# Differential attention and routed experts: the scores of four head groups made in one step, two score tiles at a time

## The chip, the cores and the metric

The kernel runs on one core of a Trainium2 chip. The metric is device time in microseconds (us) for one launch. Three runs of the kernel before took 1216.85, 1217.22 and 1220.14 us, so its median is 1217.22 us.

The engines are named as the profile names them: PE is TensorE with its matmuls, PEld is TensorE's weight load, DVE is VectorE, ACT is ScalarE, POOL is GpSimd and SP is SyncE. PSUM is the memory that TensorE writes its products into.

## The reference

The input x is 8 sequences of 512 tokens with 128 features. One layer of attention with 16 heads of 8 features makes two score matrices per head, takes two softmaxes, subtracts one from the other and divides by the sum of absolute values. A residual and a layer norm follow. Then each token goes to the best two of 8 experts, again with a residual and a norm.

```python
q = _split_heads(x @ Wq.T); k1 = _split_heads(x @ Wk1.T); k2 = _split_heads(x @ Wk2.T)
s1 = jnp.einsum('bhqd,bhkd->bhqk', q, k1) * SCALE
s2 = jnp.einsum('bhqd,bhkd->bhqk', q, k2) * SCALE
attn_exp, attn_noise = softmax(causal(s1)), softmax(causal(s2))
attn = attn_exp - sigmoid(lambda_logit) * attn_noise
attn = attn / jnp.maximum(jnp.sum(jnp.abs(attn), -1, keepdims=True), 1e-06)
out = jnp.einsum('bhqk,bhkd->bhqd', attn, v)
...
h = jax.nn.silu(jnp.einsum('btd,edf->betf', xn, W1))
y = jnp.einsum('betf,efd->betd', h, W2)
out = jnp.einsum('bte,betd->btd', wdense, y)
```

## The kernel before

**Units.** The attention is cut into 128 units: 8 batches, and in each 16 blocks of 32 queries (class `Unit`, L294). Block j sees L = 32(j+1) keys. The 16 heads lie in four groups g of 32 rows; the four heads of a group, times 32 queries, fill the 128 partitions of a result. A unit has eight score matrices of 128 x L, one for each group and each of the two key sets s.

**Slots.** The scores of a unit are made in slots, each with its own PSUM tile `sc` of 128 x 2 x 512 float32, from a pool of two (`ps_s`, L121). For L up to 256 (early units, tiles named sc_None in the profile) a slot is one pair of groups with both key sets, and a unit has two. For L above 256 (late units, tiles named sc) a slot is one pair of groups with one key set, and a unit has four. `scores` (L312) issues two products for a slot (L327), each of which uses 32 rows of TensorE, and two small products that add the causal mask (L336). Each product in float32 shows as two records in the profile.

**The way of a unit.** `maxima` (L345) takes the negated maximum of a slot on DVE (L349 early, L357 late). `exps` (L361) makes the exponentials on ACT into the tile `et` (L367), with their sums. `ratios` (L375) makes the factor c2 from the sums, three small DVE instructions. `combine` (L385) takes one piece of the unit: DVE finds the larger of the two softmaxes for the sum of absolute values (L393), and POOL scales the second set by -c2 (L403) and gathers leftover blocks (L417). `transposes` (L439) turns and adds both sets on PE into the single PSUM tile `pt` (L448). `evacuate` (L458) copies it with ACT (L473). `times_v` (L480) multiplies by the values on PE (L490). After each fourth unit `block_tasks` (L498) copies the sums of products (L508), normalises, projects and adds the residual.

**Order.** The order on every engine is written out by hand: the engines take instructions in the order in which Python issues them. `round_of` (L1083) is one round, for the slot `now`; it issues the scores of the next slot, `ahead`, and moves every unit that is on its way by one step. Steps that have been queued run in it at fixed places: `on_act` on ACT, `on_dve` and `on_dve_late` on DVE, `on_pool`, `moves` and `gathers` on POOL. Its last part issues tasks of other work: `misc` (projections of the next batch, L236, and the steps of a block), `routing`, and the experts (`turn`, L866; `hidden`, L897). How many expert tasks are issued follows from a counter `due`, which grows by a modelled time of the round (L1131 to L1140), not from a clock.

The order inside a round before the change, cut short:

```python
after_blocks(...)                                   # times_v of finished units
ahead["sc"] = ahead["u"].scores(ahead["slot"])
v.evacuate(piece, pt); run(on_act)
now["u"].maxima(now["slot"], now["sc"])
v.transposes(piece); run(on_dve)
v.combine(piece)
now["u"].exps(now["slot"], now["sc"])
```

**After the attention**, rounds without a slot drain what is left: expert tiles, the dense experts of the last two blocks, gathers and the output.

Of the kernel before, what the change touches and what calls it, by code (L numbers as in the profile page):

```python
# [9 lines left out]
F32 = mybir.dt.float32  # L10
# [10 lines left out]
def kernel(  # L21
# [16 lines left out]
    P = 128  # L38
    B, T, D = x.shape
# [4 lines left out]
    Q = 32  # L44
# [67 lines left out]
    with ExitStack() as actx:  # L112
# [181 lines left out]
        class Unit:  # L294


            def __init__(self, b, j, blk):
                self.b, self.j, self.blk = b, j, blk
                self.L = (j + 1) * Q
                self.n = -(-self.L // P)  # L300
                self.i, self.jj = j // JT, j % JT

                self.early = self.L <= T // 2
                self.slots = [(gp, None) for gp in range(2)] if self.early else [
                    (gp, s) for gp in range(2) for s in range(2)
                ]
                self.pieces = [(0, 1), (2, 3)] if self.early else [(g,) for g in range(NG)]
                self.nm = sp.tile([P, NG, 2], F32, tag="nm", name=f"nm_{b}_{j}")
                self.et = ep.tile([P, NG, 2, T], F32, tag="et", name=f"et_{b}_{j}")
                self.aT = self.c2 = self.rest = None  # L310

            def scores(self, slot):  # L312
                gp, s = slot
                qb, kT = qkv[self.b][:2]
                L, j = self.L, self.j
                sc = ps_s.tile([P, 2, T], F32, tag="sc", name=f"sc_{self.b}_{j}_{gp}_{s}")

                if s is None:
                    parts = [sc[:, gi].rearrange("p (s l) -> p s l", s=2) for gi in range(2)]
                    sets = slice(0, 2)  # L320
                else:
                    parts = [sc[:, gi : gi + 1] for gi in range(2)]
                    sets = slice(s, s + 1)
                ns = sets.stop - sets.start
                for gi in range(2):
                    r = slice(32 * (2 * gp + gi), 32 * (2 * gp + gi) + 32)
                    nc.tensor.matmul(  # L327
                        parts[gi][:, :, :L],
                        lhsT=qb[r, j].rearrange("p h q -> p (h q)"),
                        rhs=kT[r, sets, :L],  # L330
                        start=True,
                        stop=False,
                    )
                for gi in range(2):
                    r = slice(32 * (2 * gp + gi), 32 * (2 * gp + gi) + 32)
                    nc.tensor.matmul(  # L336
                        parts[gi][:, :, L - Q : L],
                        lhsT=i4[r].rearrange("p h q -> p (h q)"),
                        rhs=mk[r].unsqueeze(1).to_broadcast([32, ns, Q]),
                        start=False,  # L340
                        stop=True,
                    )
                return sc

            def maxima(self, slot, sc):  # L345
                gp, s = slot
# [38 lines left out]
            def combine(self, piece):  # L385

                if self.c2 is None:
                    self.ratios()  # L390
                L = self.L
                for g in piece:
                    nc.vector.scalar_tensor_tensor(  # L393
# [649 lines left out]
                step()  # L1043

        misc, routing, experts, moves, gathers = (deque() for _ in range(5))
        to_combine, to_transpose, to_evacuate, to_multiply = deque(), deque(), deque(), deque()

        def after_blocks(u):
            u.times_v()
# [10 lines left out]
        def time_of(width):  # L1060

            return (0.5 + width / 1024) / 1.5
# [17 lines left out]
        pace = due = now_at = 0.0  # L1080
        attention_done = False

        def round_of(now=None, ahead=None):  # L1083

            nonlocal due, now_at
            for _ in range(len(to_multiply)):
                after_blocks(to_multiply.popleft())
            if ahead:  # L1090
                ahead["sc"] = ahead["u"].scores(ahead["slot"])
            for _ in range(len(to_evacuate)):
                v, piece, pt = to_evacuate.popleft()
                v.evacuate(piece, pt)
                if piece[-1] == NG - 1:
                    to_multiply.append(v)
            run(on_act)
            if now:
                now["u"].maxima(now["slot"], now["sc"])
            for _ in range(len(to_transpose)):  # L1100
                v, piece = to_transpose.popleft()
                to_evacuate.append((v, piece, v.transposes(piece)))
            run(on_dve)
            left = now["left"] if now else 2
            for _ in range(-(-len(to_combine) // left)):
                v, piece = to_combine.popleft()
                v.combine(piece)
                to_transpose.append((v, piece))
            if now:
                now["u"].exps(now["slot"], now["sc"])  # L1110
                if now["left"] == 1:
                    to_combine.extend((now["u"], piece) for piece in now["u"].pieces)
            run(on_dve_late)
            room = 2
            if misc:
                misc.popleft()()
                room -= 1
            if routing:
                step = routing.popleft()
                step()  # L1120
                room -= step.__name__ == "counts"


            for _ in range(1 if now else 2):
                if on_pool:
                    on_pool.popleft()()
                elif moves:
                    moves.popleft()()
                elif gathers and (now or not misc and not routing):
                    gathers.popleft()()  # L1130
            if now:  # L1131
                spent = time_of(2 * now["u"].L * (2 if now["slot"][1] is None else 1))
                now_at += spent
                due += spent * pace
            else:
                due += 2
            while due >= 1 and experts and room:
                experts.popleft()()
                due -= 1
                room -= 1  # L1140
            due = min(due, 4.0)

        with tc.manual_schedule(
# [57 lines left out]
                        zero.unsqueeze(1).to_broadcast([P, c.nt, D]),  # L1201
                    )

            last = None
            for b in range(B):
                for j in range(NJ):
                    if j % JT == 0:
# [7 lines left out]
                    if b + 1 < B and j == 8:  # L1215
                        misc.extend(projection_tasks(b + 1))
                    u = Unit(b, j, blk)
                    for k, slot in enumerate(u.slots):
                        ahead = {"u": u, "slot": slot, "left": len(u.slots) - k}
                        if last is None:  # L1220
                            ahead["sc"] = u.scores(slot)
                        else:
                            round_of(last, ahead)
                        last = ahead
            round_of(last)
            attention_done = True
            while (
                to_combine or to_transpose or to_evacuate or to_multiply
                or misc or routing or experts or moves or gathers or on_act or on_dve or on_dve_late or on_pool
            ):  # L1230
                round_of()
# [49 lines left out]
```

## Time and profile before

| | us |
|---|---|
| three runs | 1216.85, 1217.22, 1220.14 |
| profiled execution, own time | 1212.04 |
| span of that execution's trace | 1210.1 |
| PE busy | 1093.9 |
| DVE busy | 927.1 |
| ACT busy | 780.4 |
| POOL busy | 526.8 |
| mean granted TensorE clock | 0.927 of full speed |

The durations below come from the profiled execution, so sums are made against its time, 1212.04 us, of which the trace covers 1210.1 us. It lies 0.4% below the median of the three runs. A busy PE is not PE at its peak, since matmuls are pipelined and their ends are modelled in the trace.

In a group of instructions of the profile, `out<-in` names the tiles, then come the shapes, the count, the busy time in us, the mean duration of one in ns, and the idle time of the engine just before these instructions with what ended most of it. In a timeline each line has its start in us, its length in us, the engine, the line of code and the operation; a count behind x means that many records merged in one line. Windows give, for each stretch, the busy time of PE, PEld, DVE, ACT and POOL with instruction counts, and then the granted clock, the busy share of the DMA engines and GB/s.

### The profile page before, as it was taken

How to read it: one execution, taken by the hardware profiler on the slowest of the kernel's cores; microseconds unless marked ns; L12 is line 12 of the kernel's file. 1: busy time of each engine (PE TensorE's matmuls, PEld its weight loads, DVE VectorE, ACT ScalarE, POOL GpSimd, SP SyncE). 2: the span in 40 equal slices, each digit the busy share in tenths (PEclk: the TensorE clock that was granted, in tenths of full speed). 3: DMA queues.
4: the chain of work that ended last, by engine and by line, in shares of the span. 5: the costliest groups of instructions: out<-in, count | busy, mean ns of one | idle time of the engine just before them, and what ended most of it. 6: DMA issues, size and time to landing. Idle time of an engine off the chain costs nothing.

```text
span 1210.1 us, 28192 instructions
## 1 busy us (share of the span) xinstructions
PE 1093.9 (90%) x9450; PEld 776.2 (64%) x9450; DVE 927.1 (77%) x2837; ACT 780.4 (64%) x2775; POOL 526.8 (44%) x935
## 2 busy tenths in 40 slices
PE   5999899989999899989998999988999989997686
PEld 3566565555666566666666666666667667777675
DVE  4688778777887887987887878887767898874556
ACT  3678767576777777766766867774567566662221
POOL 4343433463423442267464432333554652444333
PEclk7699969797999999989998999997899799998998
DMA  4400000110221112100322222221213344444762
GB/s 133 122 8 1 10 2 8 31 56 30 50 63 46 54 32 67 45 27 27 93 69 58 73 54 68 64 73 31 81 52 91 95 120 124 122 123 129 207 177 67
DMA packets 128895, 84.28 MB, mean 70 GB/s; under 512 B 22896, under 2 KB 114288, under 8 KB 128752
## 3 DMA queue, kind: packets, MB, share of 16 engines
q1 hardware_dynamic: 111952, 68.26, 20.2%
q0 software_dynamic: 3840, 7.87, 2.3%
q10 hardware_dynamic: 12960, 6.36, 1.8%
q8 instruction: 75, 1.23, 0.4%
q14 instruction: 68, 0.56, 0.2%
HBM read 63.31 MB, written 17.56 MB: 67 GB/s over the span
## 4 chain that ended last, share of the span: by engine, by line
PE 60%; DVE 16%; ACT 11%; issue 6%; POOL 4%; DMA 3%; ACTq 1%; POOLq 0%; SPq 0%; DVEq 0%
PE pt L448 19%; PE sc L327 13%; ACT et L367 7%; PE po L490 5%; PE pz L900 5%; PE pa L880 5%; PE sc_None L327 5%; DVE junk L393 2%; DVE nm L357 2%; PE pmo L541 2%; ACT aT L473 2%; DVE nm L349 2%; POOL et L403 1%; DVE hT L847 1%; POOL xs L777 1%
## 5 line engine op out<-in xcount | busy, mean ns | idle before, releaser
L403 POOL TENSOR_SCALAR et<-et,c 128x224 f32<-128x224 f32 (+15 forms) x512 | 270.9, 534 | 458.1 <-DVE junk L393 295.0
L448 PE MATMUL pt<-ident,et 128*128 128x128 f32 (+1 forms) x2048 | 326.7, 296 | 26.8 <-ACT aT L473 14.9
L448 PEld LDWEIGHTS pt<-ident,et 128*128 128x128 f32 (+1 forms) x2048 | 230.5, 145 | 159.6 <-issue 58.2
L367 ACT ACTIVATE et<-sc,nm 128x512 f32<-128x512 f32 (+7 forms) x512 | 300.4, 595 | 48.7 <-DVE nm L357 27.6
L357 DVE TENSOR_REDUCE nm<-sc 128x2 f32<-128x576 f32 (+7 forms) x256 | 252.0, 984 | 45.1 <-PE sc L336 44.6
L473 ACT COPY aT<-pt 128x384 f32<-128x384 f32 (+5 forms) x488 | 186.1, 407 | 134.5 <-PE pt L448 130.7
L393 DVE SCALAR_TENSOR_TENSOR junk<-et,c 128x224 f32<-128x224 f32 (+15 forms) x512 | 258.6, 505 | 9.6
L327 PE MATMUL sc<-kT,qb 32*128 32x384 f32 (+7 forms) x1024 | 246.8, 559 | 10.9 <-ACT et L367 9.6
L367 ACT ACTIVATE et<-sc_None,nm 128x256 f32<-128x256 f32 (+7 forms) x512 | 188.6, 387 | 32.0 <-DVE nm L349 22.0
L327 PE MATMUL sc_None<-kT,qb 32*128 32x512 f32 (+7 forms) x512 | 116.5, 535 | 21.8 <-ACT et L367 21.0
L900 PE MATMUL pz<-xgT,w 128*128 128x128 f32 x704 | 102.1, 291 | 18.8 <-DVE xgT L874 18.5
L349 DVE TENSOR_REDUCE nm<-sc_None 128x4 f32<-128x256 f32 (+7 forms) x128 | 96.1, 751 | 29.6 <-PE sc_None L336 29.3
L327 PEld LDWEIGHTS sc<-kT,qb 32*128 32x128 f32 x1024 | 78.3, 187 | 61.3 <-ACT et L367 27.4
L367 ACT ACTIVATION_READ_ACCUMULATOR et<-sc_None,nm 128x1 f32 x512 | 108.1, 211 | 0.0
L900 PEld LDWEIGHTS pz<-xgT,w 128*128 128x128 f32 x704 | 92.5, 204 | 23.6 <-DVE xgT L874 21.2
L367 ACT ACTIVATION_READ_ACCUMULATOR et<-sc,nm 128x1 f32 x512 | 103.9, 203 | 0.0
L880 PE MATMUL pa<-w,hT 128*128 128x128 f32 x704 | 98.1, 285 | 0.6 <-ACT ysb L890 0.6
L845 ACT ACTIVATE th<-pz 128x512 f32<-128x512 f32 x88 | 52.7, 599 | 68.9 <-PE pz L900 47.9
L880 PEld LDWEIGHTS pa<-w,hT 128*128 128x128 f32 x704 | 90.9, 202 | 1.3 <-ACT ysb L890 0.7
L777 POOL DMA_INDIRECT xs<-xh,row x60 | 65.9, 1099 | 46.9 <-DMA xs<-xh,row 31.3
L490 PE MATMUL po<-aT,vt 128*32 128x128 f32 (+1 forms) x2048 | 85.3, 290 | 0.0
L847 DVE SCALAR_TENSOR_TENSOR hT<-th,pz 128x512 f32<-128x512 f32 x88 | 60.2, 684 | 30.8 <-ACT th L845 30.6
(150 smaller groups left out, 1281.0 us busy)
## 6 DMA issues: line engine op xcount, KB each, us to landing
w<-in_w_dram SPq DMA_DIRECT2D x192, 256.0 KB
xg<-xs SPq DMA_DIRECT2D x88, 64.0 KB
ys<-ysb ACTq DMA_DIRECT2D x88, 64.0 KB
xs<-zero SPq DMA_DIRECT2D x2, 1600.0 KB
xs<-zero SPq DMA_DIRECT2D x2, 1216.0 KB
xt<-in_x_dram SPq DMA_DIRECT2D x8, 256.0 KB
out_dram<-ot SPq DMA_DIRECT2D x32, 64.0 KB
vr<-vt SPq DMA_DIRECT2D x32, 32.0 KB
```

What stands on the lines that cost most here:

```text
L327: nc.tensor.matmul(parts[gi][:, :, :L], lhsT=qb[r, j].rearrange("p h q -> p (h q)"), rhs=kT[r, sets, :L], start=True, stop=False,)
L349: nc.vector.tensor_reduce(self.nm[:, g, :], sc.rearrange("p g (s l) -> p g s l", s=2)[:, :, :, : self.L], AX.X, ALU.max, negate=True,)
L357: nc.vector.tensor_reduce(self.nm[:, g, s], sc[:, :, : self.L], AX.X, ALU.max, negate=True)
L367: nc.scalar.activation(self.et[:, g, si, : self.L], sc[:, gi, lo : lo + self.L], AF.Exp, bias=self.nm[:, g, si : si + 1], accum_out=self.b ...
L393: nc.vector.scalar_tensor_tensor(junk[:, :L], self.et[:, g, 1, :L], self.c2[:, g : g + 1], self.et[:, g, 0, :L], ALU.mult, ALU.max, accum_ ...
L403: nc.gpsimd.tensor_scalar(self.et[:, g, 1, :L], self.et[:, g, 1, :L], self.c2[:, g : g + 1], -1.0, ALU.mult, ALU.mult,)
L448: nc.tensor.matmul(pt[: len(gs) * kw, x_, :], lhsT=lhsT, rhs=ident, is_transpose=True, start=(k == 0), stop=(k == 1),)
L473: nc.scalar.copy(self.aT[: rows[done], self.used + done : self.used + end, :], pt[: rows[done], done:end, :],)
L490: nc.tensor.matmul(self.blk["po"][32 * g : 32 * g + 32, self.jj, :], lhsT=v[:rows, kb, 32 * g : 32 * g + 32], rhs=self.aT[:rows, self.at[g ...
L777: nc.gpsimd.indirect_dma_start(ch.xs[:, :], bass.IndirectOffsetOnAxis(ap=ch.row[:, k, c : c + 1], axis=0), ch.xh[:, c, :], None,)
L880: nc.tensor.matmul(pm[:, 1, :], lhsT=hT[y][:, f, :], rhs=w[y][1][:, f, :], start=(f == 0), stop=(f == NF - 1),)
L900: nc.tensor.matmul(pz[:, f, :], lhsT=w[t][0][:, f * P : (f + 1) * P], rhs=xgT[t], start=True, stop=True,)
```

## The change

The scores of a unit are no longer made slot by slot, one slot ahead. `scores` now takes a key set (or both, early), allocates both `sc` tiles, and issues the four products of all groups in a row, then the four masks. The slots of a late unit are reordered so that the two slots of one key set stand next to each other. A pair of rounds now shares one call of `scores`, at the head of its first round; both maxima follow in that round; the exponentials stay one slot per round. Scores are no longer issued in the round before their own.

Inside a round the queued DVE work and the combination now stand ahead of the maxima. The ratios leave `combine` and are issued in the first round of the next unit, behind its maxima; the pieces enter the queue only then, so each is combined, transposed, copied and multiplied by the values one round later. How many pieces a round takes is counted anew.

```diff
-                self.slots = [...] if self.early else [(gp, s) for gp in range(2) for s in range(2)]
+                self.slots = [...] if self.early else [(gp, s) for s in range(2) for gp in range(2)]
...
-            def scores(self, slot):
-                gp, s = slot
+            def scores(self, s):
...
-                sc = ps_s.tile([P, 2, T], F32, tag="sc", name=f"sc_{self.b}_{j}_{gp}_{s}")
+                tiles = [
+                    ps_s.tile([P, 2, T], F32, tag="sc", name=f"sc_{self.b}_{self.j}_{gp}_{s}")
+                    for gp in range(2)
+                ]
...
-                for gi in range(2):
-                    r = slice(32 * (2 * gp + gi), 32 * (2 * gp + gi) + 32)
+                for g in range(NG):
+                    r = slice(32 * g, 32 * g + 32)
                     nc.tensor.matmul(
-                        parts[gi][:, :, :L],
+                        parts[g][:, :, :L],
...
-                if self.c2 is None:
-                    self.ratios()
...
-        def round_of(now=None, ahead=None):
+        def combining(n):
+            for _ in range(min(n, len(to_combine))):
+                v, piece = to_combine.popleft()
+                v.combine(piece)
+                to_transpose.append((v, piece))
+
+        def round_of(now=None, pair=None):
...
+            if pair:
+                pair["sc"] = pair["u"].scores(pair["s"])
             for _ in range(len(to_multiply)):
                 after_blocks(to_multiply.popleft())
-            if ahead:
-                ahead["sc"] = ahead["u"].scores(ahead["slot"])
...
             run(on_act)
-            if now:
-                now["u"].maxima(now["slot"], now["sc"])
...
             run(on_dve)
-            left = now["left"] if now else 2
-            for _ in range(-(-len(to_combine) // left)):
...
+                rounds = now["of"] - now["k"] + 1 if now["k"] else 1
+            else:
+                rounds = 2
+            combining(-(-len(to_combine) // rounds))
+            if pair:
+                for k in range(2):
+                    pair["u"].maxima(pair["slots"][k], pair["sc"][k])
             if now:
-                now["u"].exps(now["slot"], now["sc"])
-                if now["left"] == 1:
-                    to_combine.extend((now["u"], piece) for piece in now["u"].pieces)
+                k = now["k"]
+                now["u"].exps(now["u"].slots[k], now["pair"]["sc"][k % 2])
+            if to_divide and not (now and now["k"]):
+                v = to_divide.popleft()
+                v.ratios()
+                to_combine.extend((v, piece) for piece in v.pieces)
+            if now and k == now["of"] - 1:
+                to_divide.append(now["u"])
             run(on_dve_late)
...
+                    of = len(u.slots)
+                    for k in range(of):
+                        if k % 2 == 0:
+                            pair = {"u": u, "s": u.slots[k][1], "slots": u.slots[k : k + 2]}
+                        round_of({"u": u, "k": k, "of": of, "pair": pair}, None if k % 2 else pair)
```

The tasks at the end of a round, the pacing of the experts, all pools and their sizes are as before.

## The prediction

> **What bounds the kernel now.** I read the engine shares first, then the chain of waits, then the table by stretches, and last the timeline of a few rounds.
>
> ```profile
> PE 1093.9 (90%) x9450; PEld 776.2 (64%) x9450; DVE 927.1 (77%) x2837; ACT 780.4 (64%) x2775; POOL 526.8 (44%) x935
> PE 60%; DVE 16%; ACT 11%; issue 6%; POOL 4%; DMA 3%; ACTq 1%; POOLq 0%; SPq 0%; DVEq 0%
> PE pt L448 19%; PE sc L327 13%; ACT et L367 7%; PE po L490 5%; PE pz L900 5%; PE pa L880 5%; PE sc_None L327 5%; DVE junk L393 2%; DVE nm L357 2%; PE pmo L541 2%; ACT aT L473 2%; DVE nm L349 2%; POOL et L403 1%; DVE hT L847 1%; POOL xs L777 1%
> ```
>
> TensorE is named for 60% of the chain, and the score products (L327, both forms) for 13% + 5% of 1210.1 us, 218 us. By these lines alone, halving the products would bring 109 us.
>
> Next the stretches, cut at the first exponential of a batch and of its ninth query block: batch 0 early and late, batch 4 early and late, and what follows the last exponential.
>
> ```profile
> 19.30:60.70 41.40, 37.97 (x223) 21.55 (x225) 27.27 (x108) 28.95 (x145) 14.97 (x36) 0.58 0.54 150
> 60.70:130.10 69.40, 67.95 (x628) 43.35 (x622) 58.94 (x154) 55.31 (x174) 26.73 (x46) 1.00 0.02 4
> 512.60:564.30 51.70, 44.34 (x384) 30.42 (x385) 40.85 (x152) 34.57 (x157) 34.62 (x57) 0.90 0.08 26
> 564.30:647.20 82.90, 78.69 (x711) 54.42 (x707) 71.52 (x195) 58.81 (x183) 47.29 (x68) 0.98 0.27 75
> 1089.10:1210.10 121.00, 86.90 (x634) 78.77 (x634) 67.31 (x202) 28.57 (x56) 43.93 (x53) 0.91 0.52 145
> ```
>
> After window and length come busy TensorE, weight load, VectorE, ScalarE, GpSimd, the granted clock, DMA. A late block in batch 4 takes 82.9/8 = 10.4 us; its TensorE is busy 95%, but VectorE is at 86% and ScalarE at 71%, so nothing has much room. Over all batches the same cut gives 682 us for 64 late blocks (5.33 us per pair of rounds) and 388 us for 64 early ones (6.06 us, one pair each): 1070 us from the first exponential (19.3) to the last (1089.1), 121 us behind it.
>
> ```profile
> 606.13 0.87 PE L448 MATMUL pt<-ident,et 128*128 128x128 f32 x6
> 606.25 1.03 DVE L357 TENSOR_REDUCE nm<-sc 128x2 f32<-128x832 f32 x1 [0.86 <-PE sc L336]
> ...
> 607.04 0.48 ACT L473 COPY aT<-pt 128x384 f32<-128x384 f32 x1 [0.79 <-PE pt L448]
> ...
> 607.05 1.02 PE L327 MATMUL sc<-kT,qb 32*128 32x448 f32 x4
> ...
> 607.42 0.61 ACT L367 ACTIVATE et<-sc,nm 128x416 f32<-128x416 f32 x1
> ...
> 607.90 0.18 PE L336 MATMUL sc<-mk,i 32*128 32x32 bf16 x2
> ...
> 608.01 0.61 ACT L367 ACTIVATE et<-sc,nm 128x416 f32<-128x416 f32 x1
> ...
> 608.13 1.09 DVE L357 TENSOR_REDUCE nm<-sc 128x2 f32<-128x896 f32 x1
> ...
> 608.50 0.21 ACT L367 ACTIVATION_READ_ACCUMULATOR et<-sc,nm 128x1 f32 x1
> ```
>
> ```profile
> L367 ACT ACTIVATE et<-sc,nm 128x512 f32<-128x512 f32 (+7 forms) x512 | 300.4, 595 | 48.7 <-DVE nm L357 27.6
> L357 DVE TENSOR_REDUCE nm<-sc 128x2 f32<-128x576 f32 (+7 forms) x256 | 252.0, 984 | 45.1 <-PE sc L336 44.6
> L367 ACT ACTIVATE et<-sc_None,nm 128x256 f32<-128x256 f32 (+7 forms) x512 | 188.6, 387 | 32.0 <-DVE nm L349 22.0
> L349 DVE TENSOR_REDUCE nm<-sc_None 128x4 f32<-128x256 f32 (+7 forms) x128 | 96.1, 751 | 29.6 <-PE sc_None L336 29.3
> ```
>
> In the timeline the reader is to see two score tiles at work at once. While ScalarE reads one (607.42 to 608.71), TensorE fills the other (607.05) and VectorE starts its maximum at 608.13. So the order products, maximum, exponentials of one tile is covered by the other's. The four groups give the mean durations used below, late (sc) and early (sc_None).
>
> **What the change does to this cover.** Each round pair now writes both tiles together. There are still two buffers, so nothing of the next pair can be complete before both tiles of this one have been read. In the instruction order of the changed kernel a pair is: TensorE four products, four masks, one transposition, tasks, then a second transposition, tasks; VectorE queued work, combination, both maxima; ScalarE copy, exponentials of tile 0, copy, exponentials of tile 1. Products on the second tile wait for ScalarE's last exponential; the masks stand behind them, the maxima behind the masks. That is a closed ring.
>
> **Its length, late** (128 pairs, mean width 400). Release to product 0.11 us (an exponential's readout ends at 608.71, the next products start at 608.82, in the same timeline). Product start to maximum 1.00 (605.22 to 606.25 is 1.03 at width 416). Maximum 0.98 (L357, 252.0 us/256). To the first exponential 0.14 (607.28 to 607.42). Two exponentials 2 x 0.595 + 0.10 for the last readout = 1.29. The copy between, until the next exponential starts, 0.45 (0.38 at 607.04 plus its start). Two more exponentials 1.29. Sum **5.26 us**, x128 = 673 us.
>
> **Early** (64 pairs, product width 288). 0.11 + 0.82 (1.03 less 128 columns at 1.7 ns, from L327's forms: 640 ns at 512, 506 at 352, two passes) + 0.75 (L349) + 0.14 + 4 x 0.387 + 0.10 = 1.65, copy 0.40, another 1.65: **5.52 us**, x64 = 353 us. Both: 1026 us, already near the 1070 of now, before anything else hangs on the ring.
>
> **What hangs on it.**
> - ScalarE jobs that fall between the two groups of exponentials, counted in the new order: 32 tanh x 0.60, 30 output copies x (0.27 + 0.33 to issue their DMA, by the timeline), 7 key copies x 0.60, 31 copies of the raw output x 0.59: 60 us. In the other half of the pair they lie under products and maximum and cost nothing.
> - TensorE's second transposition waits for the copy after tile 0 and ends about 0.25 us before the exponentials of tile 1 do. A heavy task behind it (about 0.9 us for four products of L880 or L900) makes the next products late by 0.55. The order has 53 in late pairs; a third is covered by the ScalarE jobs above. About 25 us, with the loaded last batches. In early pairs four exponentials cover it.
> - VectorE work ahead of the maxima. The combination (0.51 + 0.08) fits under the products, but queued work stands before it now, where the maximum used to come first. xgT (0.41), the normalised output (0.69) or the query copy (0.69) that waits for a task just before the products makes the maximum 0.2 to 0.8 us late, some 70 times, and mixing (two of 0.35 plus statistics) where VectorE is full: 40 us.
> - The granted clock is 0.927, so some 15% of pairs run at half rate: 28 x (0.7 more in the products, about 0.5 in the transposition): 35 us.
> - Batch starts, where narrow blocks carry the wide transpositions of the batch before: 10 us, guessed from 6.65 and 5.74 us that blocks of width 32 and 64 take now.
>
> Sum 1026 + 170 = 1196 us against 1070. TensorE's own demand (5.33 - 0.91 = 4.4 us a late pair) no longer binds. Combining a round later removes no instruction: 512 combinations and 128 ratios stay, GpSimd's scaling gets a round more of slack, and et has three buffers, enough by the order. No DMA is added or removed; those of a tile's task still go with it on SP and ScalarE, and GpSimd's gathers keep their place behind the scaling. Nor does work leave the end: 19 of 88 hidden-layer tasks and all dense ones stay behind the last scores, as now, so the 121 us stay. Span 1210 + 126 = 1336, own time (1212.04 now) 1338; the median of the runs is 1.0043 times the profiled run, which makes 1344. I take **1340 us**, a little down for the masks' order: if masks of the already finished tile pass beside the running products, up to 0.25 us a pair (48 us) comes back.
>
> **Two rules against the rows.** No row shows four products side by side. The row shows two: one record of width 448 lasts 628 ns, and four of them (two products of two passes each) fit into 1.02 us. The Trainium skill, "TensorEngine Tiling (Array Packing)", section Theoretical Speedup, gives up to 4x for a contraction of at most 32. By the rule four take about 1.0 us; by the row taken as a limit, two after two, 0.7 us more late and 0.5 early, 121 us in all. I take the rule, since two already run beside each other without loss.
> The rule that speaks against the change is in "Perfetto Trace Analysis", section Matmuls: independent groups should rotate through PSUM banks, so that the reading of one overlaps the next group's products. The row agrees for now (608.13 above). By the product row alone the sum is -109 us; by the rule, with the overlap gone, it is the ring's +126. I take the ring, because the waits stand in the new order.
>
> **Rivals.**
> - Relief wins (10%): the tasks, transpositions and products were the limit, and the ring is shorter than TensorE's 4.4 us a late pair. Then 109 us go: 1212 - 109, as a median about 1108. For it: TensorE busy 95% in late stretches. Against: four exponentials and a maximum alone are 3.6 us, to which products and the copy must be added. It decides only where the late pair is below 5.3.
> - The clock falls (12%): TensorE, idle more, is granted half rate in 40% of pairs instead of 15%: 48 more x 1.7 us (with tasks) = +82, 1422. For it: 0.58 in batch 0's early stretch. Against: 1.00 right behind it.
> - The four do not run together (6%): +121, 1461.
> - The pieces cancel (4%): ring as computed, half of the 170 hidden: 1217 to 1255.
> - The forecast (68%): 1270 to 1410.
>
> A measurement tells 0.3% from no change. The range 1235 to 1440 takes in the forecast, most of the clock case and the masks' gain. Faster 0.10, same 0.03, slower 0.87.
>
> **What would show it.** Right: the products at about half their present share; TensorE waiting on ScalarE's exponentials at L367 before nearly every pair; VectorE waiting on masks before the first maximum of each pair; ScalarE waiting on the maximum; TensorE busy near 75%, late pairs near 6 us. Wrong: a late pair under 5.3 us, or eight records of a pair spread over 1.7 us instead of 1.1, or a tail other than 121 us.

## The result and the profile after

The changed kernel takes 1335.62 us (median of four runs, 1335.11 to 1336.38), the kernel before, on the same chips, 1217.03 (median of four, 1208.66 to 1220.14). The ratio is 1.0987, with a 95% interval of 1.0932 to 1.1042: slower by 9 to 10%.

Engine shares and the chain of waits, from the page of the changed kernel:

```profile
PE 1017.0 (76%) x9450; PEld 755.8 (57%) x9450; DVE 923.7 (69%) x2837; ACT 758.8 (57%) x2775; POOL 538.7 (40%) x935
PE 38%; DVE 27%; ACT 20%; issue 8%; POOL 4%; DMA 2%; ACTq 0%; POOLq 0%; SPq 0%; DVEq 0%
ACT et L373 14%; PE pt L452 13%; DVE nm L363 10%; PE sc L333 7%; DVE junk L397 4%; ACT aT L477 4%; PE sc_None L333 4%; PE pa L884 4%; PE pz L904 4%; DVE nm L355 3%; PE po L494 2%; PE pmr L530 1%; POOL l_rs L567 1%; DVE x L939 1%; POOL got L929 1%
```

TensorE went from 90% busy to 76%, and from 60% of the chain to 38%. The score products are 11% of a longer span, where they were 18%. Their place on the chain is taken by exponentials (14%, from 7% at the late ones) and maxima (13%, from 4%): the chain now goes round through three engines.

The groups that show it, with their idle time and its cause in the last column:

```profile
L452 PE MATMUL pt<-ident,et 128*128 128x128 f32 (+1 forms) x2048 | 335.8, 305 | 231.1 <-ACT aT L477 229.8
L373 ACT ACTIVATE et<-sc,nm 128x512 f32<-128x512 f32 (+7 forms) x512 | 301.2, 598 | 261.6 <-DVE nm L363 231.8
L363 DVE TENSOR_REDUCE nm<-sc 128x2 f32<-128x576 f32 (+7 forms) x256 | 241.5, 985 | 95.5 <-PE sc L342 94.7
L373 ACT ACTIVATE et<-sc_None,nm 128x256 f32<-128x256 f32 (+7 forms) x512 | 188.8, 391 | 124.3 <-DVE nm L355 113.2
L333 PE MATMUL sc<-kT,qb 32*128 32x384 f32 (+7 forms) x1024 | 166.2, 611 | 4.4 <-ACT et L373 4.2
L333 PE MATMUL sc_None<-kT,qb 32*128 32x512 f32 (+7 forms) x512 | 85.8, 575 | 11.4 <-ACT et L373 9.8
```

The transpositions and the score products in the kernel before:

```profile
L448 PE MATMUL pt<-ident,et 128*128 128x128 f32 (+1 forms) x2048 | 326.7, 296 | 26.8 <-ACT aT L473 14.9
L327 PE MATMUL sc<-kT,qb 32*128 32x384 f32 (+7 forms) x1024 | 246.8, 559 | 10.9 <-ACT et L367 9.6
L327 PE MATMUL sc_None<-kT,qb 32*128 32x512 f32 (+7 forms) x512 | 116.5, 535 | 21.8 <-ACT et L367 21.0
```

The mean durations of exponentials and maxima have hardly moved (598 ns for 595, 985 for 984). What moved is the idle time: ScalarE stands 262 us ahead of late exponentials, where it stood 49 us, and TensorE 231 us ahead of transpositions, where it stood 27 us. The busy time of the score products fell from 246.8 to 166.2 us (late) and from 116.5 to 85.8 us (early), 111 us in all, and more than that went into waits.

TensorE's waits do not stand where the prediction named them. Ahead of its score products it waits less for exponentials than before: 14.0 us (4.2 + 9.8) where it was 30.6 (9.6 + 21.0). It waits ahead of transpositions, for a copy by ScalarE to empty `pt`. Sorted by their place, these waits fall on the second transposition of a pair (233 us, 165 waits) and hardly on the first (1 us): the second one needs the copy that stands behind the exponentials of the first tile.

The stretches from the first exponential to the last and from there to the end, with the columns as before:

```profile
19.20:1221.40 1202.20, 924.21 (x8778) 675.73 (x8778) 849.65 (x2613) 727.05 (x2714) 485.79 (x799) 0.89 0.19 54
1221.40:1334.10 112.70, 84.28 (x642) 75.71 (x642) 67.36 (x202) 29.16 (x58) 43.72 (x53) 0.94 0.56 156
```

The whole loss lies in the attention: 1202 us, where it was 1070. The end got 8 us shorter. One pair of a late unit, from the timeline:

```profile
695.00 1.03 PE L333 MATMUL sc<-kT,qb 32*128 32x448 f32 x6
695.10 0.23 ACT L373 ACTIVATION_READ_ACCUMULATOR et<-sc,nm 128x1 f32 x1
695.19 0.50 ACT L477 COPY aT<-pt 128x384 f32<-128x384 f32 x1
...
695.85 0.18 PE L342 MATMUL sc<-mk,i 32*128 32x32 bf16 x2
695.86 0.54 PE L333 MATMUL sc<-kT,qb 32*128 32x448 f32 x2
...
696.24 0.18 PE L342 MATMUL sc<-mk,i 32*128 32x32 bf16 x2
...
696.47 2.09 DVE L363 TENSOR_REDUCE nm<-sc 128x2 f32<-128x896 f32 x2 [1.57 <-PE sc L342]
...
697.65 0.63 ACT L373 ACTIVATE et<-sc,nm 128x448 f32<-128x448 f32 x1 [1.96 <-DVE nm L363]
```

The last exponential of the pair before is read out at 695.33. The second tile's products follow at once, the two maxima run back to back from 696.47, and ScalarE, done with its copy at 695.69, stands for 1.96 us. Nobody fills another score tile meanwhile, because there is none. Here the products of the first tile started ahead of the others, since that tile was free earlier; so the four did not run side by side in this pair.

The first maximum starts at 696.47, 0.07 us behind the end of the last product (696.40), and not behind the masks of its own tile, which the trace draws as ending at 696.03; their signal came at 696.44. This is general: in none of the 192 pairs does the first maximum start before the last product record ends; the least distance is 0.06 us.

From readout to first maximum this pair took 1.14 us, and the mean of late pairs is 1.89. A slower one:

```profile
705.87 1.33 PE L452 MATMUL pt<-ident,et 128*128 128x128 f32 x6 [1.99 <-ACT aT L477]
706.99 1.06 PE L530 MATMUL pmr<-ident,rexp 128*128 128x128 f32 x4
...
707.98 1.84 PE L333 MATMUL sc<-kT,qb 32*128 32x480 f32 x8
```

TensorE has waited 1.99 us for the copy. Then come the transposition and a step of a block, and the products start 0.92 us after the last readout, which ends at 707.06. So two ways lead from one pair to the next: over the readout of the second tile, and over the copy, the second transposition and TensorE's task. In 75 of 191 pairs the second tile's products follow the readout within 0.3 us; in 79 even the first tile's start later than that.

To price each stage I took the start and end of every score product, maximum and exponential out of the trace and averaged over the pairs (us; the first pair of the kernel has no predecessor):

| stage of the ring | late: forecast | late: measured | early: forecast | early: measured |
|---|---|---|---|---|
| last readout to first maximum | 1.11 | 1.89 | 0.93 | 2.00 |
| first maximum | 0.98 | 0.99 | 0.75 | 0.76 |
| to the first exponential | 0.14 | 0.06 | 0.14 | 0.09 |
| first group of exponentials | 1.29 | 1.26 | 1.65 | 1.56 |
| between the groups | 0.45 | 0.60 | 0.40 | 0.68 |
| second group | 1.29 | 1.27 | 1.65 | 1.58 |
| sum | 5.26 | 6.08 | 5.52 | 6.68 |
| pairs, total | 128, 673 | 128, 779 | 64, 353 | 63, 421 |

The forecast column is the bare ring; its additions (170 us) were listed apart and belong to the first and fifth rows.

### The profile page after: what moved, and what is told of

Same layout as the page of the kernel before. It is cut to its first block, busy times and chain, and to the rows that moved or that the text cites. A ratio compares the mean times of both kernels' runs of the same rounds, so it can differ in the third digit from the quotient of the medians.

```text
span 1334.1 us, 28087 instructions
## 1 busy us (share of the span) xinstructions
PE 1017.0 (76%) x9450; PEld 755.8 (57%) x9450; DVE 923.7 (69%) x2837; ACT 758.8 (57%) x2775; POOL 538.7 (40%) x935
## 4 chain that ended last, share of the span: by engine, by line
PE 38%; DVE 27%; ACT 20%; issue 8%; POOL 4%; DMA 2%; ACTq 0%; POOLq 0%; SPq 0%; DVEq 0%
ACT et L373 14%; PE pt L452 13%; DVE nm L363 10%; PE sc L333 7%; DVE junk L397 4%; ACT aT L477 4%; PE sc_None L333 4%; PE pa L884 4%; PE pz L904 4%; DVE nm L355 3%; PE po L494 2%; PE pmr L530 1%; POOL l_rs L567 1%; DVE x L939 1%; POOL got L929 1%
## 5 line engine op out<-in xcount | busy, mean ns | idle before, releaser
L452 PE MATMUL pt<-ident,et 128*128 128x128 f32 (+1 forms) x2048 | 335.8, 305 | 231.1 <-ACT aT L477 229.8
L407 POOL TENSOR_SCALAR et<-et,c 128x224 f32<-128x224 f32 (+15 forms) x512 | 278.2, 549 | 443.9 <-DVE junk L397 320.3
L452 PEld LDWEIGHTS pt<-ident,et 128*128 128x128 f32 (+1 forms) x2048 | 240.9, 150 | 346.9 <-ACT aT L477 276.1
L363 DVE TENSOR_REDUCE nm<-sc 128x2 f32<-128x576 f32 (+7 forms) x256 | 241.5, 985 | 95.5 <-PE sc L342 94.7
L333 PE MATMUL sc<-kT,qb 32*128 32x384 f32 (+7 forms) x1024 | 166.2, 611 | 4.4 <-ACT et L373 4.2
L355 DVE TENSOR_REDUCE nm<-sc_None 128x4 f32<-128x256 f32 (+7 forms) x128 | 90.9, 752 | 87.9 <-PE sc_None L342 87.6
L884 PEld LDWEIGHTS pa<-w,hT 128*128 128x128 f32 x704 | 95.8, 211 | 3.0 <-issue 2.2
L333 PE MATMUL sc_None<-kT,qb 32*128 32x512 f32 (+7 forms) x512 | 85.8, 575 | 11.4 <-ACT et L373 9.8
L333 PEld LDWEIGHTS sc<-kT,qb 32*128 32x128 f32 x1024 | 59.2, 202 | 42.6 <-ACT et L373 17.0
L878 DVE TENSOR_SCALAR xgT<-pa,gam,bet 128x128 f32<-128x128 f32 x88 | 35.7, 406 | 58.3 <-ACT ysb L894 54.2
```

Source lines behind the costliest of these rows:

```text
L333: nc.tensor.matmul(parts[g][:, :, :L], lhsT=qb[r, j].rearrange("p h q -> p (h q)"), rhs=kT[r, sets, :L], start=True, stop=False,)
L355: nc.vector.tensor_reduce(self.nm[:, g, :], sc.rearrange("p g (s l) -> p g s l", s=2)[:, :, :, : self.L], AX.X, ALU.max, negate=True,)
L363: nc.vector.tensor_reduce(self.nm[:, g, s], sc[:, :, : self.L], AX.X, ALU.max, negate=True)
L407: nc.gpsimd.tensor_scalar(self.et[:, g, 1, :L], self.et[:, g, 1, :L], self.c2[:, g : g + 1], -1.0, ALU.mult, ALU.mult,)
L452: nc.tensor.matmul(pt[: len(gs) * kw, x_, :], lhsT=lhsT, rhs=ident, is_transpose=True, start=(k == 0), stop=(k == 1),)
L884: nc.tensor.matmul(pm[:, 1, :], lhsT=hT[y][:, f, :], rhs=w[y][1][:, f, :], start=(f == 0), stop=(f == NF - 1),)
```

## The experiments

All ratios are to the kernel before, run beside the changed one on the same chip, with 95% intervals. Its median was 1215.6, 1222.8 and 1223.9 us beside three groups of these runs, so a difference in us between runs of different groups can be off by some 8 us.

**A longer ScalarE, in both kernels.** If exponentials stand in a ring, one more of them must show; if they are covered, it must not.

```diff
+                        if g == 3 and si == (s or 0):
+                            nc.scalar.activation(self.et[:, g, si, : self.L], sc[:, gi, lo : lo + self.L],
+                                AF.Exp, bias=self.nm[:, g, si : si + 1])
                         nc.scalar.activation(
```

In the changed kernel:

> The changed kernel with one exponential more per pair of rounds on ScalarE (the last group's is made twice, same result): 0.60 us in 128 late pairs and 0.39 us in 64 early ones, 102 us of ScalarE work. Theory (the exponentials are in the ring): nearly all of it shows, 80 to 105 us, 1415 to 1440 us. Rival (TensorE or VectorE sets the pace): ScalarE is busy 57% only, so 0 to 30 us, under 1366 us.

Measured 1397.4 us, ratio 1.1506 (1.1453 to 1.1559): 62 us over the changed kernel. This lies between the two expectations, somewhat nearer the ring. In its trace a late pair takes 6.43 us for 6.08, so 0.35 of the 0.60 shows; the stretch from readout to maximum fell from 1.89 to 1.57. The longer exponentials cover part of what had made the products and maxima late. So most of ScalarE's time counts, as in a ring, but about 0.3 us a pair of TensorE's and VectorE's own lateness is in it too.

In the kernel before:

> The kernel before with the same extra exponential, as many of them (102 us of ScalarE work). Theory (two score tiles in turn cover ScalarE's work, TensorE sets the pace in the late stretches): less than half shows, 15 to 50 us, 1232 to 1267 us. Rival (the exponentials were on the path of the kernel before as well, so the ring is nothing new): 80 us or more, over 1297 us.

Measured 1255.14 us, ratio 1.0335 (1.0283 to 1.0388), 40 us more. The theory holds: 102 us of ScalarE work cost 40 where two tiles alternate and 62 in the ring. The difference is smaller than I had thought; ScalarE is not free in the kernel before either.

**Two by two instead of four.** Products and masks of the first tile, then of the second.

```diff
-                for g in range(NG):
+                for gp in range(2):
+                    for g in (2 * gp, 2 * gp + 1):
                         nc.tensor.matmul(parts[g][:, :, :L], ...)
-                for g in range(NG):
+                    for g in (2 * gp, 2 * gp + 1):
                         nc.tensor.matmul(parts[g][:, :, L - Q : L], ...)
```

> The changed kernel with the four products no longer in a row: products and masks of the first tile, then products and masks of the second, at the same place in the order. Two products side by side instead of four, and the first maximum no longer stands behind the release of the second tile. Theory (the ring sets the pace, TensorE has room): not slower; 0 to 35 us shorter, 1300 to 1337 us, because in some 51 of 191 pairs TensorE stands ready more than 0.3 us before the last exponential ends and the maximum can then start earlier. Rival (four side by side is worth TensorE's time): 0.9 us more in 128 late pairs and 0.6 in 64 early ones, 150 us, near 1480 us; half of it, 1410, if half is hidden.

Measured 1297.04 us, ratio 1.0684 (1.0631 to 1.0738): 39 us faster than the changed kernel, slightly more than expected. Readout to first maximum fell to 1.68 us in late pairs and 1.66 in early ones. The form that the change is named for, four in a row, costs time in this schedule: the first maximum has to stand behind the release, and behind the products, of a tile that it doesn't read. With two by two it starts before the last product's end in 65 of 192 pairs, with four in a row in none. Where four do run together, they take the time of two, so the loss is not theirs:

```profile
715.80 1.09 PE L333 MATMUL sc<-kT,qb 32*128 32x480 f32 x8
```

Eight records (four products of two passes) of width 480 take 1.09 us, where four records of width 448 took 1.02 in the kernel before.

**Maxima first on VectorE.**

```diff
             run(on_act)
+            if pair:
+                for k in range(2):
+                    pair["u"].maxima(pair["slots"][k], pair["sc"][k])
             for _ in range(len(to_transpose)):
```

> The changed kernel with both maxima issued on VectorE straight behind the scores of their pair, ahead of the queued work and of the combination; nothing else differs. In the trace of the changed kernel the first maximum starts on average 0.27 us after its masks end in late pairs and 0.31 us in early ones, 47 us over all pairs, because VectorE is still busy. Theory (a ring of products, maximum, exponentials sets the pace, and this lag is a part of it): 20 to 45 us shorter than 1335.6, so 1290 to 1315 us. Rival (VectorE's total is what counts, the order only moves work around): 1325 to 1345 us. Rival 2 (the combination, now behind the maxima, makes scaling and transpositions late): above 1345 us.

Measured 1488.89 us, ratio 1.226 (1.2177 to 1.2344), slower by far: my theory was wrong and the second rival right. The lag between masks and maximum did vanish (0.06 us late, 0.04 early), and the products got later instead (readout to maximum 2.34 us). In its timeline:

```profile
701.80 1.42 DVE L363 TENSOR_REDUCE nm<-sc 128x2 f32<-128x576 f32 x2 [1.97 <-PE sc L342]
...
703.65 0.45 DVE L397 SCALAR_TENSOR_TENSOR junk<-et,c 128x224 f32<-128x224 f32 x1
...
704.28 1.07 POOL L407 TENSOR_SCALAR et<-et,c 128x224 f32<-128x224 f32 x2 [3.00 <-DVE junk L397]
...
704.98 0.98 PE L452 MATMUL pt<-ident,et 128*128 128x128 f32 x7 [0.23 <-POOL et L407]
...
705.94 1.14 PE L884 MATMUL pa<-w,hT 128*128 128x128 f32 x8
...
707.01 0.77 PE L333 MATMUL sc<-kT,qb 32*128 32x288 f32 x8
```

Both maxima hold VectorE, the combination starts behind them, GpSimd scales behind the combination, the transposition waits for GpSimd, an expert task stands behind it, and only then come the next products. This is a second, longer ring. That the change puts the combination ahead of the maxima is thus needed by the pair order, at 47 us of lag.

**The copy out of the ring.** The transposition of a first round is copied before the exponentials, not between them.

```diff
-                to_evacuate.append((v, piece, v.transposes(piece)))
+                pt = v.transposes(piece)
+                if pair:
+                    v.evacuate(piece, pt)
+                    if piece[-1] == NG - 1: to_multiply.append(v)
+                else:
+                    to_evacuate.append((v, piece, pt))
```

> The changed kernel with the copy of the first round's transposition issued on ScalarE ahead of that round's exponentials, not between the two groups of exponentials; the second transposition then finds its PSUM tile free. Theory (the copy stands in the ring, and TensorE's tasks at the end of a pair make products late only because the transposition ahead of them waits for this copy): the stretch between the two groups of exponentials falls from 0.60 to about 0.25 us in late pairs, the products are less late, 50 to 110 us shorter, 1225 to 1285 us. Rival (the copy now waits for the transposition behind the products and holds up the exponentials by as much): 1320 to 1350 us.

Measured 1266.7 us, ratio 1.0396 (1.032 to 1.0472), 69 us faster than the changed kernel. The stretch between the groups fell from 0.60 to 0.27 us, as forecast, readout to maximum to 1.68 (1.65 in early pairs), and 0.14 us came back ahead of the first group, which now waits for the copy. In late pairs both parts of the theory stand. In early pairs the rival is right about the copy: 0.46 us left the stretch between the groups (0.68 to 0.22) and 0.47 came back ahead of the first group (0.09 to 0.56), so that their gain is in the earlier products alone.

With two by two as well:

> The last edit (copy ahead of the exponentials) on the kernel with products and masks tile by tile (1297 us). Theory (both are parts of one ring and add up): 50 to 100 us under 1297, 1197 to 1247 us, about the kernel before. Rival (the tile-by-tile order already took what the copy would give): 1270 to 1300 us.

Measured 1248.01 us, ratio 1.0217 (1.017 to 1.0265): 49 us under two by two (57 by the ratios): at the lower edge of the theory and clear of the rival. Alone the two edits gave 39 and 69 us, together 88, so they share some 15 to 20 us. The late pair takes 5.59 us.

**TensorE's tasks ahead of the next products.** First I moved the second round's tasks ahead of its transposition:

```diff
             run(on_dve)
+            if now and not pair:
+                run(on_dve_late)
+                tasks_of_round(now)      # misc, routing, on_pool, experts
             for _ in range(len(to_transpose)):
```

> The changed kernel with the tasks of a pair's second round (experts, projections, steps of a block) issued on TensorE ahead of that round's transposition instead of behind it, so none stands just ahead of the next products; their DVE and ScalarE parts follow in the next round as before. In the trace of the changed kernel the products of 57 of 128 late pairs and 22 of 63 early ones begin more than 0.3 us after the last exponential, and these pairs have their first maximum 1.0 to 1.7 us later than the others: some 95 us, where 25 had been forecast for TensorE's tasks. Theory (these tasks are the cause): 40 to 90 us shorter, 1245 to 1295 us. Rival (the products are late for another reason, for instance because the second transposition itself is late): within 20 us of 1335.

Measured 1349.93 us, ratio 1.1046 (1.1002 to 1.1089): no gain, the rival's range. The tasks' inputs come from VectorE and GpSimd, which are not done with them at that place (TensorE waits 52 us for `rexp` at L530, where it waited 13), and now the transposition waits behind the tasks:

```profile
708.69 1.01 PE L530 MATMUL pmr<-ident,rexp 128*128 128x128 f32 x4 [3.03 <-POOL rexp L525]
...
709.49 1.49 PE L452 MATMUL pt<-ident,et 128*128 128x128 f32 x6
...
710.91 1.73 PE L333 MATMUL sc<-kT,qb 32*128 32x480 f32 x8
```

So this edit added a wait and tells nothing of the tasks' own price. The second try issues experts in first rounds only:

```diff
-            while due >= 1 and experts and room:
+            while due >= 1 and experts and room and (pair or not now):
```

> The changed kernel with expert tasks issued only in the first round of a pair (and after the attention); other tasks stay. So no expert product stands between the second transposition and the next pair's scores, and none has been moved ahead of a transposition. 26 hidden-layer tasks instead of 19 are left behind the attention, so the end gets some 15 to 20 us longer and only the stretch from the first to the last exponential (1202 us in the changed kernel) tells. Theory (expert products just ahead of the scores hold the pair up; the trace puts 72 us on them): that stretch 40 to 75 us shorter, 1127 to 1162 us; in all 1280 to 1315 us. Rival (the lateness moves to other waits, as when tasks went ahead of the transposition): that stretch above 1185 us.

Measured 1319.24 us, ratio 1.0797 (1.0698 to 1.0896). From first to last exponential it takes 1164.6 us, 38 less than the changed kernel, and the end 134.5 us, 22 more. The gain lies just under the theory's range and clear of the rival's. Readout to maximum fell by 0.45 us in late pairs and 0.40 in early ones, 82 us together; the stretch between the groups grew by 0.24 and 0.26, 47 us, because the experts' tanh and output copies now all fall there (63 and 61 of them, where it was 32 and 30). That experts just ahead of the products hold the pair up is thus shown, and more than half of the gain is lost at another place.

**All mends together**, with ScalarE's queued work of a second round put behind its exponentials:

```diff
-            run(on_act)
+            if pair or not now:
+                run(on_act)
...
                 now["u"].exps(...)
+            run(on_act)
```

> Scores in pairs with all that shortened it: products tile by tile, the copy ahead of the exponentials, experts in the first round only, and ScalarE's queued work of the second round behind its exponentials. Theory (the ring can be cut to products, maximum and four exponentials, about 4.9 us a late pair): 30 to 60 us under the 1248 us of the two first mends, 1190 to 1220 us with the longer end; still not under the 1194 us of the kernel before with later combination, which keeps scores one slot ahead. Rival (the pair order can be mended to beat it): under 1185 us.

Measured 1273.85 us, ratio 1.0465 (1.0365 to 1.0565): a miss, 26 us slower than the two first mends alone. Most of that is the longer end, 136 us for 115, which comes with issuing experts in first rounds only. From first to last exponential both take 1112 us: the two added mends gained nothing there. The stretch between the groups is gone (0.00 us for 0.27 in late pairs), but readout to first maximum grew from 1.22 to 1.52 us. What fits is that tanh now ends late and VectorE waits for it with the next maxima behind (101 us ahead of hT, L852); no run separates this.

**The two parts of the change, each alone.** The later combination in the kernel before:

```diff
-                if self.c2 is None:
-                    self.ratios()
...
-                if now["left"] == 1:
-                    to_combine.extend((now["u"], piece) for piece in now["u"].pieces)
+            if to_divide and not (now and now["left"] < now["of"]):
+                v = to_divide.popleft()
+                v.ratios()
+                to_combine.extend((v, piece) for piece in v.pieces)
+            if now and now["left"] == 1:
+                to_divide.append(now["u"])
```

> The kernel before with the second part of the change alone: ratios in the first round of the next unit, the pieces combined, transposed and multiplied one round later; scores, maxima and exponentials stay one slot ahead as they were. Theory (the loss is the scores' alone, the later combination only adds slack): within 12 us of the kernel before, 1204 to 1228 us. Rival (the delay itself costs, for instance by crowding wide transpositions into the narrow blocks that start a batch): 20 to 60 us more, over 1235 us.

Measured 1194.06 us, ratio 0.9798 (0.9743 to 0.9853): 1.5 to 2.6% faster than the kernel before, and the fastest of all. Neither theory nor rival had this. Its waits against those of the kernel before, GpSimd's wait for the combination first here, then there:

```profile
POOL et L401 <- DVE junk L391: 210.9, 159, 4.2
```

```profile
POOL et L403 <- DVE junk L393: 295.0, 198, 4.7
```

The early stretches took 370 us for 388 and the end 115 for 121; the late stretches stayed (682 us both). The granted clock was 0.946 for 0.927 in the profiled executions, and 0.930 to 0.946 in its four runs beside 0.916 to 0.927 in those of the kernel before. That a round more of distance lets TensorE wait less for scaled pieces fits: its idle time ahead of transpositions put down to GpSimd fell from 25.7 to 16.5 us. This is less than the 29 us gained, and no run separates the rest from the clock.

The scores in pairs alone:

```diff
+                if self.c2 is None:
+                    self.ratios()
...
-            if now and k == now["of"] - 1:
-                to_divide.append(now["u"])
+            if now and k == now["of"] - 1:
+                to_combine.extend((now["u"], piece) for piece in now["u"].pieces)
```

> The first part of the change alone: scores in pairs, but ratios and pieces handed on at the end of their unit as in the kernel before, with no later round. Theory (the later combination alone gained 2%, by slack for the combination, and the pair order puts the combination ahead of the maxima, so this slack matters more here): 20 to 70 us over the changed kernel, 1355 to 1405 us. Rival (in the pair order the delay is worth nothing): 1325 to 1345 us.

Measured 1429.3 us, ratio 1.1696 (1.1597 to 1.1795), 94 us over the changed kernel (86 by the ratios): right in sign, beyond the expected range. GpSimd waits 478 us for the combination, where it waited 320.

| ratio to the kernel before | combination as before | one round later |
|---|---|---|
| scores one slot ahead | 1 | 0.980 |
| scores in pairs | 1.170 | 1.099 |

The lower row has VectorE's new order as well, with the combination ahead of the maxima; the upper row has the old one.

## Why the prediction was right

- **The ring.** The sign and the size came from it. That the pairs now go round through three engines is shown by the chain, by ScalarE's waits for maxima (345 us, where it was 50), and by the edits: copy and tile order shortened it, an exponential lengthened it, and the time followed. Maximum and exponentials came within 0.1 us of the rows they were taken from. TensorE's share (76%) and the late pair (6.08 us) came as named. No run gave the pairs a third score tile, which would have been the direct test.
- **The link that closes it.** TensorE was to wait for exponentials ahead of nearly every pair. The readout opens 75 of 191 pairs; 79 are opened later, by TensorE's own transposition and tasks, the way that the forecast took for the shorter one. The products' share of the chain was to be halved and fell from 18% to 11%.
- **Sum.** From first to last exponential 1202 us against 1196 forecast. This nearness is luck. Readout to first maximum takes 368 us over all pairs, where the bare ring and the additions that belong there (25, 40, 35 and 10 us) made 312. The other rows together lie 56 us below their forecast, most of it in the exponentials (20 us) and between the groups (24 us). The end is 113 us, not 121, one of the named signs of being wrong; with the later combination alone it is 115, with the scores in pairs alone 119, so most of this comes with the later combination.
- **VectorE ahead of the maxima.** Forecast 40 us, measured 47: in 45 late and 22 early pairs the maximum starts over 0.15 us after the last mask.
- **ScalarE between the groups.** Forecast 143 us with the copies (0.45 x 128 + 0.40 x 64 + 60), measured 120 (0.60 x 128 + 0.68 x 63).
- **TensorE's tasks behind the second transposition** were mis-sized: forecast 25 us, of which early pairs none. In 79 pairs (57 late, 22 early) the products begin over 0.3 us after the last readout, 102 us together, and 73 us of these, in 58 pairs, stand directly behind an expert's products. The step took for granted that the transposition ends 0.25 us before the exponentials and that one task follows. Issuing experts elsewhere took 82 us out of this place.
- **The clock.** The forecast took 28 pairs at half rate. At the readout that opens a pair the clock stands at half rate in 50 of 191 pairs, at the start of the products in 39. The first maximum comes 49 us later in the 50, all told, and 27 us later in the 39; both hold part of the lateness in the point above, since 31 of the 50 are also among the 79. So the size stays open between these. The clock was 0.898 over the kernel: the clock rival named the direction and overdid the size.
- **Batch starts.** Blocks of width 32 and 64 together took 2.2 us more than before, 17 us for the 10 guessed.
- **The later combination** was put at nothing as a gain. It is worth 29 us in the kernel before, and 86 to 94 in the pair order. The forecast priced its instructions and took the added slack for idle. The total doesn't miss by this, since the forecast summed the ring of the changed kernel with this slack in it and gave GpSimd's scaling no place there; but it could not have told that the first part of the change alone costs 17%.
- **Four side by side.** Right: four products take the time of two when all are ready. In 63 pairs they are not: the first tile's products start over 0.3 us before the last readout, and the second tile's follow.
- **Masks.** The reserve of up to 0.25 us a pair, for which 4 us were taken off, did not come back: no first maximum starts ahead of the last product, whatever the masks of its tile do. The two-by-two order got 39 us by moving products and masks together, so the masks' share of that is not measured.

## What to carry to other kernels

Before buying matmul time with buffers that other engines drain, write down the ring that remains: release, products, reduction, activation, release. Here, with as many tiles in a step as there are buffers, its length was the pace, whatever TensorE saved. A mean of the right size doesn't show that the right link of the ring binds; look where each engine stands. And in a schedule written out by hand, judge a step by its distance from what it waits for: the 2% here came from handing a piece on one round later, with not one instruction fewer. Of three edits that moved work "earlier", two (the maxima, TensorE's tasks) put it in front of somebody else's wait, and one (the copy) gained 69 us, because the next transposition stood waiting for it.

## What the runs showed of the hardware

Four products of 32 rows each, of width 480 and with two records each, took 1.09 us when all could start (at 715.80), about what two of width 448 took in the kernel before (1.02 us).

Masks of a finished tile brought its maximum no earlier start. At 695.85 to 696.03 they stand in the trace beside products of the other tile (695.86 to 696.40) that had been issued ahead of them. In the 55 pairs where VectorE was idle and such masks are drawn as ending over 0.15 us before the last product, the maximum that needs only these masks still started 0.06 to 0.07 us behind the last product. Ends of matmuls are modelled in the trace; the start of the engine that waits is the safer sign.

The granted clock was 0.946 with the later combination alone, 0.927 before, 0.898 after, 0.850 with maxima first and 0.839 with scores in pairs alone. TensorE's busy share does not tell it: it is 76% both at 0.898 and at 0.839. In the thirteen traces the clock stands at full or half rate for 3.41 us or multiples of it. Cut into such windows, full rate was lost 546 times, always behind a window with TensorE busy for 0.81 or less, and half rate ended 533 times, always behind one of at least 0.81. Of 270 full-rate windows under 0.44, 268 were followed by half rate; between 0.44 and 0.82 it went both ways. The eight product records of width 480 at 707.98 took 1.84 us at a mean clock of 0.57, those at 715.80 1.09 us at full rate.
